# A decoder layer on one core: score fills for the maxima split between ScalarE and VectorE, the FFN's rank product in token halves

## The chip, the cores and the metric

One core of a Trainium2 chip runs the whole program. The metric is the device time of one execution in microseconds. The work is in fp32 throughout.

## The reference

Sixteen sequences of 512 tokens and 256 channels go through one decoder layer. With everything that doesn't matter here cut away, it is

```python
x = layernorm(x + attn_block(x))     # short convolution, long convolution, gate, gated MLP of 672
x = layernorm(x + xattn(x, ctx))     # 16 heads of 16: causal self-attention + attention to 64 context rows
x = layernorm(x + ffn(x))            # P = x@U1 (rank 64); H = gelu(P@V1 + b1) (1024); (H@U2)@V2 + b2

# inside xattn, per head (q and k of 16 channels, scale 1/4)
att  = where(causal, q @ k.T, -inf) * scale ;  y  = softmax(att)  @ v      # 512 x 512
attc =               qc @ kc.T      * scale ;  y += softmax(attc) @ vc     # 512 x 64
return y @ Wp + bp
```

The softmax subtracts the row's maximum, so every row of scores needs a maximum before its exponentials can be taken. The kernel makes the scores twice: once with queries in the rows, to find the maxima along the free direction (the max fills), and once with keys in the rows, with the maximum already subtracted by an extra channel of the query, to take exponentials that feed the next product (the exp fills).

## The kernel before

A front part (lines 434 to 1049, about the first 300 us) computes the projections, the short and the long convolution for all sixteen sequences. The main part then works a sequence ("batch" b) at a time: `first_block` (output projection, residual, gated MLP, layer norm), `attention`, `ffn`. No loop sets the order. Each step is an operation `plan.op(name, engines, cost, fn, prio, r=, w=, ...)` of a planner (class `Plan`, line 100). It holds a cost in microseconds for each operation, a priority (plus an offset from the table `RANKS`, line 27, by part and name), and which tiles it reads and writes. `schedule` runs a list schedule over the five engines with these costs, gives out the tiles of each pool, and `emit` issues the instructions in that order. On the chip each engine then goes through its instructions strictly in this order and waits on semaphores.

Matmuls are issued in one of four shapes of TensorE's array, written rows*columns in the profile: the whole (128*128, `FULL`), four strips of 32 columns (128*32, `STRIPS`), eight tiles of 32*64 (`ROWS`, for scores: each head has 32 rows) and eight of 64*32 (`BOTH`). Matmuls in different tiles of one shape run side by side. An operation with `flex=True` takes the whole array or strips, whichever the engine is in. `Plan.empty` (line 118) prices a change of shape; `HOLD` and `STAY` (line 1095) weigh against changing.

PSUM has eight banks of 128 x 512: one `scores` tile of four, one `av`, three `mm` (lines 1058 to 1060). All score fills of all batches use the one scores tile in turn.

`maxima(g)` (line 1472) handles a group of four heads, `g` of four groups per batch, in three fills of 512 columns for each of the four heads: query blocks 1 and 0 with their context columns, block 2 with its context and block 3's context, and block 3 alone. For batches 2 to 12 VectorE adds the causal mask in PSUM ("mask", line 1550) and reduces from PSUM ("max", line 1580). For batches 0, 1, 13, 14 and 15 (`COPIED`, line 1915) ScalarE copies all four banks into an `ex` tile ("copy", line 1525), GpSimd masks the diagonal there ("mask copy", line 1532) and VectorE reduces from the copy. In batches 0, 1 and 15 (`HALVED_MAX`) fill and copy are cut into two halves of the columns. `shifted(g)` (line 1584) turns the maxima of two groups into rows on TensorE and adds them to the queries; `sums` (line 1617) does the exp fills, the exponentials on ScalarE (line 1611), the causal triangle on GpSimd (line 1659) and the sums over keys. `divided` (line 1765) sends sums through DRAM and divides on GpSimd (lines 1804 and 1809); its numerators and inverses lie in two of three `nd` tiles.

`ffn` (line 1834): `x2T` is the transposed input; "rank" multiplies by `u1_s`, in which the 64 columns of U1 stand twice, so that `pT` (128 rows, 512 tokens) holds the ranks in both halves of its rows; "hidden" makes two blocks of 128 hidden channels at a time, one from each half of the rows; "gelu" (line 1876) takes 512 tokens of one block; "low" and "wide" are the two products back. The gelus and exponentials of the batches alternate in windows, since each needs its own table on ScalarE.

Of the kernel before, what the change touches and what calls it, by code (L numbers as in the profile page):

```python
# [8 lines left out]
F32 = mybir.dt.float32  # L9
# [18 lines left out]
    "context.sum ctx": -2000,  # L28
    "divided.num from": -400,
    "ffn.gelu": 4000,  # L30
    "ffn.hidden": -2000,
    "ffn.norm": 5000,
    "ffn.rank": -1000,
    "ffn.stats": 2000,
    "ffn.turn": -100,
    "ffn.wide": 4000,
    "first.load x": 2000,
    "first.out": -2000,
    "first.residual": -2000,
    "maxima0.max": -7000,  # L40
    "maxima1.copy": 1000,
    "maxima1.mask copy": -1000,
    "maxima1.max": -900,
    "mlp.down": 1000,
    "mlp.shift": -3000,
    "queries0.proj out": -320,
    "queries1.proj": 20,
    "queries1.proj out": -3000,
    "result.norm": 13000,
    "result.shift": 10000,  # L50
    "result.stats": 3000,
    "result.tokens": 14000,
    "shifted.max turn": 400,
    "shifted.shifted": 1000,
    "sums.exp": -1000,
    "sums.fill": -3000,
    "sums.sum": -2000,
    "sums.sum out": 2000,
    "values.ctx keys": 400,
    "values.ctx v out": 1000,  # L60
    "values.turn": -1000,
    "values.v": 100,
}
SLOT_OF = (1, 0, 2, 3)


class Buf:


    def __init__(self, cls):  # L70
        self.cls, self.seen, self.left, self.slot, self.t = cls, [], 0, None, None

# [27 lines left out]
class Plan:  # L100
# [55 lines left out]
    def matmul(self, out, weights, moving, **kw):  # L156

        rows, cols = self.now
        n = weights.shape[-1]
        for c in range(0, n, cols):  # L160
            cs = slice(c, min(c + cols, n))
            self.nc.tensor.matmul(out[cs], weights[:, cs], moving, **kw)  # L162
# [97 lines left out]
def decoder_layer(  # L260
# [60 lines left out]
    mask_qk = const.tile([P, P], F32, name="mask_qk")  # L321
    nc.gpsimd.memset(mask_qk, 0.0)
    nc.gpsimd.affine_select(
        out=mask_qk, in_=mask_qk, compare_op=ALU.is_ge, fill=NEG, base=0,
        pattern=[[-1, P]], channel_multiplier=1,
    )
# [100 lines left out]

    R8 = 8
# [5 lines left out]
    with ExitStack() as front:  # L434
# [40 lines left out]
        ramp_i = fp_.tile([P, P], I32, name="ramp_i")  # L475
        steps = fp_.tile([P, P], F32, name="steps")
        ramp = fp_.tile([P, P], F32, name="ramp")
        back = fp_.tile([P, 1], F32, name="back")
# [472 lines left out]
        u1_s = weights.tile([P, KD, 2, RANK], F32, name="u1_s")  # L951
        v1_s = weights.tile([P, NH // 2 * P], F32, name="v1_s")
        v2_s = weights.tile([P, D], F32, name="v2_s")
        v1_halves = v1.rearrange("r (p s n) -> s r p n", s=2, n=P)
        for n in range(2):
            half = bass.ts(n, RANK)
            fetch(u1_s[:, :, n, :], u1.rearrange("(k p) f -> p k f", p=P))
            fetch(v1_s[half, :].rearrange("r (p n) -> r p n", n=P), v1_halves[n])
            fetch(v2_s[half, :], v2)
        u1_s = u1_s.rearrange("p k s f -> p k (s f)")  # L960
# [110 lines left out]
        "row": tiles(kept, "row", 6, [P, T]),  # L1071
        "q": tiles(kept, "q", 11, [P, T]),
        "keys": tiles(kept, "keys", 5, [P, TC + T]),
        "kcs": tiles(kept, "kcs", 2, [P, 2, G, TC]),
        "ctx2": tiles(kept, "ctx2", 2, [CC, 2, TC]),
# [5 lines left out]
        "dk": dks,  # L1081
        "junk": tiles(kept, "junk", 1, [P, D]),
# [9 lines left out]
    for t in pool["maxes"]:  # L1092
        nc.gpsimd.memset(t, 0.0)

    plan = Plan(pool, 13890, 6870, nc, RANKS)
# [73 lines left out]
    def first_block(b, after):  # L1169
# [56 lines left out]
        if b:  # L1226
            scale_ops(y1, sq, p0, "ACT")
            zT = transposed(y1, lambda t: t, p0)
# [15 lines left out]
        for f in range(NF):  # L1244
            halves = []
            for w in (w_l1, w_l2):
                ps = Buf("mm")
                for k in range(KD):

                    def mm(e, f=f, w=w, k=k, ps=ps):  # L1250
                        plan.matmul(
                            ps.t, w[:, k, bass.ts(f, P)], zT.t[:, k, :], start=(k == 0), stop=(k == KD - 1)
# [24 lines left out]
        def mm_e(e, ps=ps):  # L1277
            for n, w in enumerate((w_l1, w_l2)):
                for k in range(KD):
                    for c in range(NT):  # L1280
                        plan.matmul(
                            ps.t[bass.ts(c, FE), bass.ts(n, P)], w[:, k, NF * P :], zT.t[:, k, bass.ts(c, P)],
# [32 lines left out]
    def attention(b, x_):  # L1315
# [3 lines left out]
        xT = transposed(x_, lambda t: t, p0)  # L1319
# [120 lines left out]
        def queries(g):  # L1440
# [29 lines left out]
            )  # L1470

        def maxima(g):

# [544 lines left out]
```

## Time and profile before

| | before |
|---|---|
| median of 3 runs | 2025.77 us (2019.52 to 2025.89) |
| profiled execution: time, span | 2020.74 us, 2018.6 us |
| mean granted TensorE clock | 0.992 |
| busy: TensorE, VectorE, ScalarE, GpSimd | 1946.6, 1320.4, 1046.4, 767.2 us |
| max reduces on VectorE, from PSUM and from copies | 311.1 us in 264, 140.6 us in 120 |
| masks on VectorE, in PSUM | 115.6 us in 132 |
| copies of scores on ScalarE | 114.3 us in 96 |
| exponentials on ScalarE | 362.7 us in 228 |

In a row of the profile, "x" is a count, "busy" the summed time of a group, "mean ns" the length of one instruction, and what follows the last bar is the idle time of the engine just before those instructions with what ended it. A line number can be that of a helper: line 162 issues most matmuls, so groups there are told apart by tiles and shapes. An fp32 matmul leaves two records.

### The profile page before, as it was taken

The numbers are of one execution on the slowest core, as the hardware profiler recorded it, in microseconds if no ns is written. First come the engines' busy times: TensorE is split into PE (matmuls) and PEld (weight loads), VectorE is DVE, ScalarE is ACT, GpSimd is POOL, SyncE is SP. The second block draws the span as 40 slices with busy tenths as digits, with TensorE's granted clock in tenths as the row PEclk, the third lists the DMA queues.
The fourth block names the chain that finished last, engine by engine and source line by source line (L and its number), as shares of the span: only waits on it lengthen the run. The fifth ranks groups of instructions, "written<-read, shape, count | busy, mean of one in ns | idle before, by whom it ended". The sixth has DMA issues, their size and how long they took to land. (4 is left out here: it accounts for less than half of the span.)

```text
span 2018.6 us, 63455 instructions
## 1 busy us (share of the span) xinstructions
PE 1946.6 (96%) x28134; PEld 864.7 (43%) x28134; DVE 1320.4 (65%) x1907; ACT 1046.4 (52%) x1478; POOL 767.2 (38%) x1036
## 2 busy tenths in 40 slices
PE   7999978999999999999999999999999999999997
PEld 4445645444444443434343434343434343434442
DVE  7987542556576757676767667676767575656564
ACT  6863521566536362636363545444444546656774
POOL 7685622243423242414242423333332324424442
PEclk9999989999999999999999999999999999999999
DMA  5375871031304131313132222222231313131200
GB/s 191 123 212 172 274 256 48 13 104 38 116 21 133 29 121 41 113 50 112 51 102 60 94 69 81 82 74 89 61 102 52 106 38 108 28 103 39 83 23 32
DMA packets 115043, 183.92 MB, mean 91 GB/s; under 512 B 13393, under 2 KB 62034, under 8 KB 114642
## 3 DMA queue, kind: packets, MB, share of 16 engines
q1 hardware_dynamic: 113234, 177.26, 27.9%
q8 instruction: 220, 3.60, 0.7%
q10 hardware_dynamic: 1536, 2.62, 0.4%
q14 instruction: 53, 0.43, 0.1%
HBM read 111.09 MB, written 68.76 MB: 89 GB/s over the span
## 5 line engine op out<-in xcount | busy, mean ns | idle before, releaser
L1611 ACT ACTIVATE ex<-scores 128x2048 f32<-128x2048 f32 (+1 forms) x228 | 362.7, 1607 | 181.3 <-PE scores L162 177.7
L1659 POOL TENSOR_SCALAR_AFFINE_SELECT ex<-ex 128x512 f32<-128x512 f32 x256 | 158.6, 634 | 498.9 <-ACT ex L1611 498.8
L162 PE MATMUL mm<-xT,w_l 128*32 128x512 f32 (+2 forms) x2940 | 316.5, 540 | 0.0
L1580 DVE TENSOR_REDUCE maxes<-scores 128x8 f32<-128x512 f32 (+4 forms) x264 | 311.1, 1220 | 4.5
L162 PE MATMUL scores<-keys,q 32*64 32x192 f32 (+5 forms) x5696 | 218.1, 407 | 9.5 <-ACT ex L1525 5.0
L162 PE MATMUL scores<-q,keys 32*64 32x256 f32 (+3 forms) x4480 | 179.9, 420 | 6.2 <-ACT ex L1611 4.8
L1548 DVE TENSOR_TENSOR scores<-scores,mask_qk 128x1024 f32<-128x1024 f32 x132 | 115.6, 875 | 106.1 <-PE scores L162 105.3
L162 PEld LDWEIGHTS scores<-keys,q 32*64 32x64 f32 x5696 | 102.9, 131 | 172.2 <-DVE maxes L1580 52.9
L162 PEld LDWEIGHTS mm<-xT,w_l 128*32 128x32 f32 (+1 forms) x2940 | 92.7, 111 | 184.6 <-issue 175.0
L162 PE MATMUL av<-ex,va 128*32 128x512 f32 (+3 forms) x2048 | 169.0, 437 | 0.1
L162 PE MATMUL mm<-w_l,gT 128*32 128x256 f32 (+1 forms) x2032 | 159.7, 381 | 0.0
L562 DVE SCALAR_TENSOR_TENSOR frow<-fmm,cw,frow 128x511 f32<-128x511 f32 x192 | 140.5, 743 | 26.0 <-ACT frow L554 21.7
L1580 DVE TENSOR_REDUCE maxes<-ex 128x4 f32<-128x512 f32 (+3 forms) x120 | 140.6, 1211 | 17.9 <-POOL ex L1532 13.7
L1804 POOL TENSOR_TENSOR nd<-nd,nd 128x1024 f32<-128x1024 f32 x30 | 71.2, 2373 | 204.5 <-DMA nd<-di 204.5
L1525 ACT COPY ex<-scores 128x1024 f32<-128x1024 f32 (+1 forms) x96 | 114.3, 1228 | 66.7 <-PE scores L162 55.9
L547 PE MATMUL fmm<-fx,inw 128*128 128x512 f32 x312 | 142.2, 598 | 0.0
L361 DVE COPY row<-av 128x512 f32<-128x512 f32 x66 | 45.6, 690 | 138.8 <-PE av L162 137.7
L1876 ACT ACTIVATE row<-mm,b_s 128x512 f32<-128x512 f32 x124 | 78.9, 685 | 102.4 <-PE mm L162 99.5
L162 PE MATMUL mm<-xT,wqc_s 128*32 128x512 f32 (+1 forms) x796 | 125.4, 595 | 0.0
L162 PEld LDWEIGHTS scores<-q,keys 32*64 32x64 f32 x4480 | 79.5, 131 | 98.6 <-ACT ex L1611 45.0
L162 PEld LDWEIGHTS mm<-w_l,gT 128*32 128x32 f32 (+1 forms) x2032 | 89.3, 117 | 68.8 <-issue 34.5
L1263 ACT ACTIVATE row<-mm 128x512 f32<-128x512 f32 x80 | 47.9, 599 | 123.7 <-PE mm L162 112.0
(201 smaller groups left out, 2954.6 us busy)
## 6 DMA issues: line engine op xcount, KB each, us to landing
dn<-row SPq DMA_DIRECT2D x120, 256.0 KB
keys<-dk SPq DMA_DIRECT2D x64, 256.0 KB
nd<-dn SPq DMA_DIRECT2D x30, 512.0 KB
nd<-di SPq DMA_DIRECT2D x30, 512.0 KB
fx<-hpad SPq DMA_DIRECT2D x28, 512.0 KB
early<-gates SPq DMA_DIRECT2D x16, 512.0 KB
early<-yconv SPq DMA_DIRECT2D x32, 256.0 KB
dk<-row SPq DMA_DIRECT2D x32, 256.0 KB
```

Source lines behind the costliest of these rows:

```text
L162: self.nc.tensor.matmul(out[cs], weights[:, cs], moving, **kw)
L361: nc.vector.tensor_copy(dst, src)
L547: nc.tensor.matmul(ps.t, inw[:, k, bass.ts(m, P)], xT.t[:, k, :], start=(k == 0), stop=(k == KD - 1))
L562: lambda e, lag=lag: nc.vector.scalar_tensor_tensor(t.t[:, lag:], ps.t[:, 0 : T - lag], cw[:, m, 2 - lag : 3 - lag], t.t[:, lag:], ALU.mul ...
L1263: lambda e, pa=pa, ge=ge: nc.scalar.activation(ge.t, pa.t, AF.Gelu_apprx_tanh),
L1525: lambda e, sc=sc, both=both, cols=cols: nc.scalar.copy(both.t[:, :, cols], sc.t[:, :, cols]),
L1548: nc.vector.tensor_tensor(diag, diag, mask, ALU.add)
L1580: nc.vector.tensor_reduce(dst, src, AX.X, ALU.max, negate=True)
L1611: lambda e: nc.scalar.activation(ex.t.rearrange("p (r n) -> p r n", r=HPG)[:, :, cols], sc.t[:, :, cols], AF.Exp, scale=scale),
L1659: lambda e, ex=ex, at=at: nc.gpsimd.affine_select(out=ex.t.rearrange("p (r n) -> p r n", r=HPG)[:, :, at : at + P], in_=ex.t.rearrange("p ...
L1804: lambda e, nums=nums, inv=inv: nc.gpsimd.tensor_tensor(nums.t, nums.t, inv.t, ALU.mult),
L1876: lambda e, f=f, s=s, bank=bank, dst=hT[s]: nc.scalar.activation(dst.t, bank(s), AF.Gelu_apprx_tanh, bias=b1_s[:, f : f + 1]),
```

## The change

In `maxima`, every batch now does the same. ScalarE copies two of the four heads (two banks) into an `nd` tile ("half"); GpSimd masks the diagonal there ("half mask"). At the same time VectorE works from the other two banks: it adds the mask to the diagonal blocks into a new small tile `part` ("mask"), reduces or folds what lies left of the diagonal into it ("off"), takes the context maxima ("max ctx"), and then, with no further use of PSUM, the own maxima from `part` ("max own") and those of the copied heads ("half ctx", "half own"). `COPIED`, `HALVED_MAX` and `SLOT_OF` go; max fills are no longer halved. `reading` tells the tile framework that the two engines read different banks, so that neither waits for the other.

In `ffn`, "rank" has U1 once and puts the first 256 tokens of a sequence into the upper half of the rows of `pT` and the last 256 into the lower half; it is always in strips. "rank out" copies 256 columns. "hidden" does a pair of channel blocks as sixteen matmuls of 256 tokens, two banks holding a token half each, and "gelu" is cut into four of 256. `v1_s` has all of V1 in both halves of its rows. The product "ctx v" of the context values makes 128 columns in strips, without the copy "twice" on GpSimd and its `ctx2` tiles. `row` tiles go from 6 to 5, `q` tiles from 11 to 10; the DMA latencies and the ranks of the planner are other numbers, and `HOLD` and `STAY` too. `turned` and the branches for `TURNED` are new code that no batch uses, since `TURNED` is empty.

```diff
-    "maxima0.max": -7000,
-    "maxima1.copy": 1000,
...
+    "maxima0.half ctx": 1000,
+    "maxima0.max own": 3000,
...
+PARTS = 1
...
-        u1_s = weights.tile([P, KD, 2, RANK], F32, name="u1_s")
-        v1_s = weights.tile([P, NH // 2 * P], F32, name="v1_s")
+        u1_s = rows(u1, "u1_s")
+        v1_s = weights.tile([P, NH * P], F32, name="v1_s")
...
-        "row": tiles(kept, "row", 6, [P, T]),
-        "q": tiles(kept, "q", 11, [P, T]),
+        "row": tiles(kept, "row", 5, [P, T]),
+        "q": tiles(kept, "q", 10, [P, T]),
...
-        "ctx2": tiles(kept, "ctx2", 2, [CC, 2, TC]),
+        "part": tiles(kept, "part", PARTS, [P, HPG // 2, 2 * P]),
...
-    plan = Plan(pool, 13890, 6870, nc, RANKS)
+    plan = Plan(pool, 13040, 5040, nc, RANKS)
...
+        def ctx_v(e, ps=ps):
+            for n in range(P // SLOT):
+                nc.tensor.matmul(
+                    ps.t[bass.ts(n, SLOT), 0:P].rearrange("p (a n) -> p a n", a=2),
+                    ctxT[:, b * TC + n % 2 * SLOT : b * TC + (n % 2 + 1) * SLOT],
+                    wcv_s.rearrange("c (a e n) -> c e a n", a=2, e=2)[:, n // 2], start=True, stop=True,
+                )
...
+            for use in (((0, TC), (1, TC)), ((2, TC), (3, None)), ((3, 0),)):
+                sc, part, half = Buf("scores"), Buf("part"), Buf("nd")
...
+                plan.op("fill", "PE", tiled(T), mm, prio, r=[q, kk], w=[(sc, 0), (sc, 1)], tiling=ROWS, urgent=True)
+                plan.op(
+                    "half", "ACT", act(two * T), lambda e, sc=sc, half=half: reading(sc, e, nc.scalar.copy(half.t, sc.t[:, two:])),
+                    prio - 6, r=[(sc, 1)], w=[half],
+                )
...
+                plan.op("half mask", "POOL", 0.4 * blocks, masked, prio - 6, w=[half])
...
+                plan.op("mask", "DVE", dve(blocks * two * P), mask, prio - 5, r=[(sc, 0)], w=[part])
+                if i0 == 0:
                     plan.op(
+                        "off", "DVE", dve(two * P),
...
+                else:
+                    reduce(
+                        "off", two * i0 * P, lambda part=part: part.t[:, :, P : P + 1],
...
+                if ctx:
+                    ctx_max("max ctx", lambda sc=sc: sc.t[:, here], here, (sc, 0), prio - 5)
...
+                        "max own", 2 * two * P, lambda: own(0, here, 2),
...
+                if ctx:
+                    ctx_max("half ctx", lambda half=half: half.t, there, half, prio - 4)
...
+                            "half own", two * n, lambda i=i: own(i, there),
...
-                plan.matmul(ps.t, u1_s[:, k, :], x2T.t[:, k, :], start=(k == 0), stop=(k == KD - 1))
-
-            plan.op("rank", "PE", pe(T), pt, p3 - k, r=[(x2T, k)], w=[ps], flex=True)
...
+                for n in range(P // SLOT):
+                    half, cols = n // 2, bass.ts(n % 2, SLOT)
...
+                        to, moving = ps.t[bass.ts(n, SLOT), 0:D], tokens(x2T, k)[:, bass.ts(half, D)]
+                    nc.tensor.matmul(to, u1_s[:, k, cols], moving, start=(k == 0), stop=(k == KD - 1))
+
+            plan.op("rank", "PE", pe(D), pt, p3 - k, r=[(x2T, k)], w=[ps], tiling=STRIPS)
...
+                for s in range(2):
+                    for c in range(0, P, SLOT):
+                        for h in range(2):
+                            half, at = bass.ts(h, RANK), (2 * fp + s) * P + c
+                            nc.tensor.matmul(
+                                bank(h)[c : c + SLOT, bass.ts(s, D)], v1_s[half, at : at + SLOT], pT.t[half, 0:D],
+                                start=True, stop=True,
+                            )
...
+                        "gelu", "ACT", act(D, True),
...
-    COPIED = (0, 1, B - 3, B - 2, B - 1)
-
-    HALVED, HALVED_MAX = (0, 1, B - 1), (0, 1, B - 1)
+    TURNED = (), (), (), ()
+
+    HALVED = (0, 1, B - 1)
```

## The prediction

> **What bounds the kernel now.** I read the page's busy table first, then the busy time by stage, then the timeline of two microseconds-long cycles in the middle, and last the groups by shape. The span of the profiled execution is 2018.6 us and its own time 2020.74 us; the median of the three timed runs is 2025.77 us. All sums below are made on 2020.74, which is 5 us under that median; about 0.3% (6 us) is what a measurement of this kernel can tell from no change.
>
> ```profile
> span 2018.6 us, 63455 instructions
> PE 1946.6 (96%) x28134; PEld 864.7 (43%) x28134; DVE 1320.4 (65%) x1907; ACT 1046.4 (52%) x1478; POOL 767.2 (38%) x1036
> ```
> ```profile
> 1000.00:1100.00 100.00, 100.00 (x1516) 41.51 (x1508) 67.73 (x97) 47.58 (x60) 33.65 (x44) 1.00 0.27 82
> 1885.00:1925.00 40.00, 36.15 (x776) 15.44 (x776) 32.98 (x37) 32.80 (x42) 17.55 (x22) 1.00 0.19 58
> ```
> In the middle (the row from 1000 us: PE, PEld, DVE, ACT, POOL, clock, DMA) TensorE is busy all 100 us at full clock, VectorE 68, ScalarE 48. Busy alone proves little, so I price its work from the timeline:
>
> ```profile
> 1001.02 1.12 PE L162 MATMUL scores<-keys,q 32*64 32x448 f32 x32
> 1002.07 0.66 PE L1591 MATMUL mm<-ident,maxes 128*128 128x128 f32 x4
> 1002.27 0.70 DVE L1548 TENSOR_TENSOR scores<-scores,mask_qk 128x512 f32<-128x512 f32 x1 [0.42 <-PE scores L162]
> 1003.00 2.36 DVE L1580 TENSOR_REDUCE maxes<-scores 128x8 f32<-128x512 f32 x2
> 1005.68 1.11 PE L162 MATMUL scores<-keys,q 32*64 32x512 f32 x16
> ...
> 1010.34 1.28 ACT L1611 ACT_TABLE_LOAD   x1 [11.40 <-DVE maxes L1580]
> ...
> 1014.09 1.12 PE L162 MATMUL scores<-q,keys 32*64 32x384 f32 x32
> ...
> 1017.43 1.12 PE L162 MATMUL scores<-q,keys 32*64 32x256 f32 x32
> ...
> 1033.00 1.04 PE L162 MATMUL mm<-xT,wk_s 128*32 128x512 f32 x8
> ...
> 1036.77 1.90 PE L162 MATMUL mm<-xT,wqc_s 128*32 128x512 f32 x16
> ```
> A matmul leaves two records, so the eight strip matmuls of a projection are x16. Sixteen records take 1.90 us, eight take 1.04: eight more cost 0.86 us, and the other 0.18 is the pipe running empty. So one k-step of 512 tokens in four strips streams 0.86 us; at 256 columns the same comparison (0.64 us for 8 records of the MLP's down product, 1.94 for 32) gives 0.43 for eight. Adding up the columns of all records at this rate gives 90 to 91 us of stream in each 100 us from 500 to 1600. The rest is the change of tile shape: the fill at 1001.02 streams 0.86 and its successor starts after 1.05 (0.19 to leave it); entering costs about 0.13. A batch lasts 104 us and has 24 fills of the scores banks, hence 24 x 0.32 = 7.7 of the 9.5 us not streamed. TensorE is really full; nothing else is close.
>
> The second resource is the one scores tile (four banks). A max fill holds it until VectorE has masked and reduced it: 1001.02 to 1005.68, 4.7 us a cycle. An exp fill cycles in 3.3 us (1014.09 to 1017.43). Twelve of each make 96 of 104 us.
>
> **The change, part by part.**
>
> *Rank product.* Before, two k-steps of 512 tokens per batch (u1 is there twice so that both halves of the rows hold the ranks); after, the same two with 256, each strip with its own tokens. 2 x (0.86 - 0.43) = 0.86 us a batch. That strips with different moving data run together is seen in the sums over keys (av from ex), which do just that at the same rate.
>
> *Context values.* One step of 256 columns becomes 128: 0.43 to 0.22, 0.21 us a batch. Together 1.08 us x 16 = **-17.3 us** of stream on the full engine. The POOL copy that it needed (16 x 0.29) goes.
>
> *Hidden and gelu.* Eight matmuls of 512 become sixteen of 256: same columns, no change. ScalarE gets 16 gelus of 256 for 8 of 512 per batch. A gelu of 512 takes 685 ns, and the slope of ScalarE is (1865 - 1015) / 1024 = 0.83 ns an element, so one of 256 is 472: +2.1 us a batch. With 48 of 100 us busy this is covered, except after the last exp, where the chain goes from hidden by gelu to the low product: two gelus 1.37, four 1.89, **+0.5**.
>
> *Maxima.* The groups:
>
> ```profile
> L1580 DVE TENSOR_REDUCE maxes<-scores 128x4 f32<-128x2048 f32 x44 | 100.9, 2293 | 1.5
> L1548 DVE TENSOR_TENSOR scores<-scores,mask_qk 128x512 f32<-128x512 f32 x88 | 61.4, 698 | 65.8 <-PE scores L162 65.8
> L1580 DVE TENSOR_REDUCE maxes<-scores 128x4 f32<-128x1024 f32 x44 | 53.5, 1215 | 0.0
> L1525 ACT COPY ex<-scores 128x1024 f32<-128x1024 f32 x72 | 69.5, 1015 | 39.0 <-PE scores L162 28.2 <-issue 10.5 <-ACT row L363 0.3
> L1532 POOL TENSOR_SCALAR_AFFINE_SELECT ex<-ex 128x512 f32<-128x512 f32 x80 | 49.7, 635 | 132.9 <-ACT ex L1525 119.6 <-PE mm L162 6.7 <-DMA nd<-di 6.5
> ```
> VectorE's fixed part is 0.15 us (681 ns for 512 elements, 1215 for 1024: 1.04 ns each). Uncopied batches (2 to 12), per head group: masks 1.23 + 2 x 0.70, reduces 7.32, sum 9.95 us in 9 instructions. After: 17 instructions, 7,172 elements, 3.74 + 3.31 + 3.01 = 10.06 us. So +0.11 a group, +0.4 a batch: nothing. In the five copied batches the masks were POOL's: 7.27 becomes 10.06, +11.2 us a batch. [...]
>
> ScalarE: 24 copies of 1.865 and 72 of 1.015 (114 us) become 192 of 1.015 (195): +5 us a batch on average, +12 in uncopied ones. POOL: 80 masks of 0.635 become 256 of about 0.41 (slope from 1024 elements at 1.09): +54 us in all. Totals: DVE 69%, ACT 57%, POOL 41%, all beside a full TensorE.
>
> The scores tile is now free after the slower of the copy (1.02) and VectorE's first half (mask 0.70, off 0.43, context 0.43: 1.56; the others 1.54 and 1.38), where it was 3.0 to 3.8. That is 12 x 1.8 = 22 us less hold a batch, and 96 becomes 74. What it gives back is only what TensorE waits for: in the middle the mean cost of a shape change lies above its median, together 0.6 us a batch. Between 0 and 0.6 x 13 = 8 us I take half, **-4**.
>
> *Where the cover is thin.* Batches 0, 1 and 15 lose their halved max fills; the halves ran back to back, so no shape change goes, and a whole fill holds the tile no longer than two copies of 1.015 did. In the last batch's maxima (row from 1885 us) VectorE is busy 33.0 of 40 us; +11.2 makes 44.2, so the stage is at least **+4.2** unless work moves out of it; ceiling 11. The first batch (maxima from 362 to 390 us, VectorE nearly full) is the same with the next batch's matmuls as filler: 0 to 9, I take **+2**.
>
> *New waits.* VectorE's half reduces stand in its queue behind POOL's mask, which stands behind POOL's 2.4 us products; behind them stand the copies that free TensorE's three mm banks. The half sits in an nd tile; a quotient trip holds two of the three. One part tile only makes VectorE wait for itself. SP's queue loses one weight load and moves nothing else. Row tiles (6 to 5) and q tiles (11 to 10) can hold back a projection; unseen in the trace, 0 to 5, I take 0. The planner's new ranks and latencies reorder all; three more or fewer shape-change pairs a batch are 16 us either way, and I take 0.
>
> Sum: -17.3 - 4 + 4.2 + 2 + 0.5 = -14.6, so 2020.7 - 14.6 = **2006 us**.
>
> **The rivals.** *A: in-order waits (slower).* POOL's long operations (two products 2.37, two sums 1.28, two biases 2.37, four others 1.28) fill about 17 of 104 us. A mask that meets one waits some 1 us: 192 x 0.17 x 1 = 33, with the nd shortage 35. If none of that is covered, TensorE's next fill waits: 2006 + 35 = 2041. It decides once over six tenths of it (21 us) reaches TensorE, 0.11 us a fill. Against: TensorE waits for scores only 0.4 us twice in two batches now, with as long an order. *B: order.* Two to three more shape changes a batch eat the stream: about 2020. For: rank is now strips only, and beside transposes that is one change more; against: 29 of its 32 k-steps were strips already (232 records of 128*32, 6 of 128*128). *C: the ends shrink too.* Between 300 and 600 us and after 1646, non-streamed time is 13 and 25 us above the middle's rate; an order that fills 15 of it gives 1991. That the split saves no stream is excluded by the av rows.
>
> **How the numbers follow.** Forecast 0.52 (2006), C 0.22 (1991), B 0.12 (2020), A 0.14 (2041). Faster by over 0.3%: 0.52 + 0.22 = 0.74; within: 0.12; slower: 0.14. C's lower end, 1985 (six more of the 38), and the forecast with +11, +9 and +5 plus no relief, 2006 + 6.8 + 7 + 5 + 4 = 2029, bound the range: 1985 to 2029 leaves out most of A and little else.
>
> **What would show it.** Right: u_s records of 256 columns at half the busy time (14 to 18 us for 31.5), stream per batch down 1 us, the batch at 103 us, fills of the max stage about 3.5 us apart, TensorE still 100% in the middle. Wrong: idle TensorE before scores fills ended by VectorE or POOL, a half mask that waits behind the products, more than 27 shape-change pairs a batch, or maxima of the last batch over 50 us.

## Result and the profile after

The changed kernel takes 2078.8 us (median; 2074.5 to 2085.1) beside 2025.8 for the kernel before on the same chip: a ratio of 1.0264, 95% interval 1.0221 to 1.0306. It is slower by about 53 us, where 2006 was forecast. The profiled execution took 2077.2 us.

The page's span and busy table, and the row of busy time from 1000 to 1100 us (PE, PEld, DVE, ACT, POOL, clock, DMA share, GB/s):

```profile
span 2075.2 us, 66287 instructions
...
PE 1951.3 (94%) x28924; PEld 866.6 (42%) x28924; DVE 1343.2 (65%) x2498; ACT 1131.6 (55%) x1683; POOL 813.4 (39%) x1196
```
```profile
1000.00:1100.00 100.00, 95.86 (x1513) 40.41 (x1514) 62.99 (x123) 57.30 (x77) 38.80 (x57) 0.98 0.25 77
```

TensorE was busy all of these 100 us before; now it idles in 4.1 of them. Its stream has shrunk as planned: the columns of all matmul records, at the 0.86 us for eight strip records of 512 that the prediction worked out (0.84 ns a column, records of tiles side by side counted once), add up to 1776.1 us before and 1758.9 after. That is -17.2 where -17.3 was forecast. What isn't streamed grew from 2018.6 - 1776.1 = 242.5 us to 2075.2 - 1758.9 = 316.3. So the loss to be explained is +73.8 us, and changes of tile shape are not it: 973 in the run before, 984 after. It is mostly waiting: TensorE is idle for 2075.2 - 1951.3 = 123.9 us where it was 2018.6 - 1946.6 = 72.0, or 51.9 more.

The timeline shows what TensorE now waits for. In a row, "[2.97 <-POOL nd L1586]" is the idle time of the engine before the instruction and what ended it. First a max fill:

```profile
1001.74 2.35 POOL L1890 TENSOR_TENSOR nd<-nd,nd 128x1024 f32<-128x1024 f32 x1 [4.96 <-DMA nd<-di]
...
1002.99 1.11 PE L164 MATMUL scores<-keys,q 32*64 32x512 f32 x16
...
1004.05 2.38 POOL L1206 TENSOR_TENSOR xt<-xt,b_s 128x1024 f32<-128x1024 f32 x1
...
1006.39 0.40 POOL L1586 TENSOR_SCALAR_AFFINE_SELECT nd<-nd 128x256 f32<-128x256 f32 x1
...
1006.83 0.95 DVE L1561 TENSOR_REDUCE maxes<-nd 128x2 f32<-128x768 f32 x1 [2.97 <-POOL nd L1586]
...
1008.03 0.95 DVE L1561 TENSOR_REDUCE part<-scores 128x2 f32<-128x768 f32 x1
...
1009.08 1.12 PE L164 MATMUL scores<-keys,q 32*64 32x192 f32 x32 [1.84 <-issue]
```

GpSimd stood 4.96 us at the quotient's product (`divide`, L1890) until the inverses landed (`nd<-di`). Behind that product came a bias add of 2.38 us, and only then the half mask. VectorE's half reduce (`maxes<-nd`, of the fill before the one at 1002.99) waited 2.97 us for that mask. What VectorE had to do for the fill at 1002.99 from its own two banks, the reduce `part<-scores` last, stood behind it in VectorE's queue; it doesn't need GpSimd at all, but it is the last reader of the scores tile. When it ended, at 1008.98, TensorE could fill again, after 1.84 us of idle. "issue" as the releaser means that the profile names nobody; the reduce's end says who it was. The second place is 70 us later. It shows the quotient's trip through DRAM, which makes GpSimd late: the denominators are loaded (`sums<-dn`, "den from" in the planner), inverted on VectorE and stored (`di<-sums`, "inverse to"); then the inverses and the numerators are loaded (`nd<-di`, "inverse from", and `nd<-dn`, "num from") for `divide`:

```profile
1062.09 0.59 SPq L1875 DMA_DIRECT2D nd<-dn  x1
...
1063.55 0.95 DVE L1865 RECIPROCAL sums<-sums 64x128 f32<-64x128 f32 x1 [2.14 <-DMA sums<-dn]
...
1064.52 0.50 SPq L1868 DMA_DIRECT2D di<-sums  x1
...
1068.53 0.59 SPq L1882 DMA_DIRECT2D nd<-di  x1
...
1075.94 2.38 POOL L1890 TENSOR_TENSOR nd<-nd,nd 128x1024 f32<-128x1024 f32 x1 [5.98 <-DMA nd<-di]
...
1079.70 2.49 POOL L1264 TENSOR_TENSOR xt<-xt,y 128x512 f32<-128x512 f32 x2
...
1082.15 1.22 POOL L1745 TENSOR_SCALAR_AFFINE_SELECT ex<-ex 128x512 f32<-128x512 f32 x2
...
1082.84 1.64 PE L164 MATMUL av<-ex,va 128*32 128x384 f32 x16 [2.30 <-POOL ex L1745]
```

The numerators' load (`nd<-dn`, 512 KB) is issued at 1062.09, the store of the inverses (`di<-sums`, 32 KB) 2.4 us behind it. The load that reads them back (`nd<-di`) goes 4.0 us after the store and lands 7.4 us later. GpSimd stands at divide for 5.98 us until then, then has the product, a sum and a residual to do, and the causal triangles that TensorE's `av` needs come last: 2.30 us of idle. Over the run TensorE's waits are:

```profile
PE av L164 <- POOL ex L1745: 19.0, 10, 3.4
PE scores L164 <- issue: 18.7, 12, 2.5
PE scores L164 <- ACT ex L1697: 12.9, 17, 1.6
```

In the same list of before the score fills' longest entries are these, and `av` never waits for the triangles:

```profile
PE scores L162 <- ACT ex L1525: 6.1, 8, 1.6
PE scores L162 <- ACT ex L1611: 5.9, 7, 1.2
```

Some short idles cost more than themselves, as the busy time around the second one shows (clock in the third column from the right):

```profile
1080.00:1083.00 3.00, 0.70 (x12) 0.16 (x8) 0.50 (x1) 1.68 (x4) 3.00 (x4) 1.00 0.76 227
1083.00:1087.00 4.00, 4.00 (x26) 2.47 (x18) 1.28 (x2) 0.72 (x2) 4.00 (x4) 0.57 0.26 89
```

After the idle of 2.30 us the granted clock is half for 3.4 of the next 4 us. The mean granted clock over the span is 0.983 where it was 0.992: (1 - 0.983) x 2075.2 = 35.3 us of clock lost against 16.1, or 19 of the 73.8. With the 51.9 us of idle that accounts for nearly all of it.

**Why the trip is late.** Part of the diff that the prediction passed over in a clause is the planner's latencies. Before, each leg of the trip was planned with 4.0 us; now sum to and den from have 1.7, inverse to 1.1, numerators and inverse from 5.7. The rank that put the numerators' load ahead of the denominators' is gone too. The new list allows 1.88 us from the store of the inverses to the load that reads them back. In the trace it is 3.3 to 4.8 us in 24 of the 30 trips (median 4.16). SyncE's queue has its waits at that load, in total, times and longest:

```profile
SPq L1882 <- DMA di<-sums: 109.1, 30, 7.4
```

The kernel's own list, with the times that the planner gave each operation, can be worked out from its code, and set beside the trace:

| | list: den from to divide, most trips | divide on the chip, mean lateness | span - 275.9 (front's list) - list's end |
|---|---|---|---|
| before | 15.7 to 16.8 us | -0.4 us | 2018.6 - 275.9 - 1743.5 = -0.8 us |
| after | 12.2 to 13.1, six of them 15.9 to 17.5 | +2.6 | 2075.2 - 275.9 - 1726.7 = 72.6 |

Lateness is the start of divide in the trace less its start in the list, both counted from ScalarE's position at that time. The chip keeps before's list to a microsecond, and falls 72.6 us behind after's.

### The profile page after: what moved, and what is told of

It is laid out like the page before. It is cut to its first block, busy times and chain, and to the rows that moved or that the text cites. A ratio compares the mean times of both kernels' runs of the same rounds, so it can differ in the third digit from the quotient of the medians.

```text
span 2075.2 us, 66287 instructions
## 1 busy us (share of the span) xinstructions
PE 1951.3 (94%) x28924; PEld 866.6 (42%) x28924; DVE 1343.2 (65%) x2498; ACT 1131.6 (55%) x1683; POOL 813.4 (39%) x1196
## 4 chain that ended last, share of the span: by engine, by line
PE 69%; DMA 13%; POOL 5%; issue 5%; DVE 4%; ACT 4%; SPq 1%; POOLq 0%; ACTq 0%; DVEq 0%
PE mm L164 32%; PE scores L164 16%; PE av L164 7%; PE fmm L582 5%; DMA nd<-di 4%; PE mm L1965 2%; DMA dn<-row 2%; ACT ex L1697 2%; PE mm L406 2%; DMA di<-sums 2%; POOL nd L1890 1%; PE fmm L842 1%; DMA sums<-dn 1%; DMA keys<-dk 1%; DMA dk<-row 1%
## 5 line engine op out<-in xcount | busy, mean ns | idle before, releaser
L1579 ACT COPY nd<-scores 128x1024 f32<-128x1024 f32 x192 | 194.6, 1014 | 304.4 <-PE scores L164 220.2
L1586 POOL TENSOR_SCALAR_AFFINE_SELECT nd<-nd 128x256 f32<-128x256 f32 x256 | 101.4, 408 | 523.8 <-ACT nd L1579 523.7
L1561 DVE TENSOR_REDUCE maxes<-nd 128x4 f32<-128x256 f32 (+4 forms) x384 | 247.0, 677 | 52.1 <-POOL nd L1586 52.1
L164 PE MATMUL scores<-keys,q 32*64 32x192 f32 (+3 forms) x5120 | 217.0, 436 | 29.5 <-issue 18.7
L164 PE MATMUL av<-ex,va 128*32 128x512 f32 (+3 forms) x2048 | 170.2, 443 | 19.2 <-POOL ex L1745 19.0
L164 PEld LDWEIGHTS scores<-keys,q 32*64 32x64 f32 x5120 | 89.4, 131 | 190.0 <-issue 111.3
L164 PE MATMUL mm<-w_l,gT 128*32 128x256 f32 (+1 forms) x2344 | 168.4, 381 | 0.0
L164 PE MATMUL mm<-xT,wqc_s 128*32 128x512 f32 (+1 forms) x874 | 123.9, 596 | 0.0
L1890 POOL TENSOR_TENSOR nd<-nd,nd 128x1024 f32<-128x1024 f32 x30 | 71.2, 2372 | 123.4 <-DMA nd<-di 123.4
L164 PEld LDWEIGHTS mm<-w_l,gT 128*32 128x32 f32 (+1 forms) x2344 | 81.1, 112 | 83.4 <-issue 43.4
L1600 DVE TENSOR_TENSOR part<-scores,mask_qk 128x256 f32<-128x256 f32 (+1 forms) x192 | 97.5, 508 | 26.9 <-PE scores L164 24.2
L1977 ACT ACTIVATE row<-mm,b_s 128x256 f32<-128x256 f32 x248 | 100.3, 476 | 26.4 <-PE mm L1965 13.3
L589 ACT ACTIVATE frow<-fmm,cb,cw 128x512 f32<-128x512 f32 x96 | 74.0, 777 | 70.3 <-PE fmm L582 52.8
```

The lines of the kernel that those rows point to most:

```text
L589: lambda e: nc.scalar.activation(t.t, ps.t, AF.Identity, bias=cb[:, m : m + 1], scale=cw[:, m, 2:3]),
L1561: inst = nc.vector.tensor_reduce(dst(), src(), AX.X, ALU.max, negate=negate)
L1579: "half", "ACT", act(two * T), lambda e, sc=sc, half=half: reading(sc, e, nc.scalar.copy(half.t, sc.t[:, two:])),
L1586: nc.gpsimd.affine_select(out=block, in_=block, compare_op=ALU.is_ge, fill=NEG, base=0, pattern=[[0, two], [-1, P]], channel_multiplier=1,)
L1600: reading(sc, e, nc.vector.tensor_tensor(to, on_diagonal(sc.t[:, here]), m, ALU.add))
L1890: lambda e, nums=nums, inv=inv: nc.gpsimd.tensor_tensor(nums.t, nums.t, inv.t, ALU.mult),
```

## The experiments

The theory: the finished order has no room for the trip, and engines that take their instructions strictly in order pay for that again and again. The first rivals: the split fills themselves cost the time, or the order does for another reason (shape changes, lack of fillers). All medians below are beside the kernel before on the same chip (2023.7 to 2025.9 us).

### Shorten or postpone the trip, keep the split

`c1_small_num` loads 32 KB of numerators instead of 512 and multiplies the inverses with themselves, so the numerators are left out of its result:

```diff
-  out=nums.t, in_=dn.t[:, 1 : 1 + HD].rearrange(...)
+  out=nums.t[:, 0, 0:64], in_=dn.t[:, 1 : 1 + HD, 0:1, 0:64].rearrange(...)
-  nc.gpsimd.tensor_tensor(nums.t, nums.t, inv.t, ALU.mult)
+  nc.gpsimd.tensor_tensor(nums.t, inv.t, inv.t, ALU.mult)
```

> The changed kernel, order of every engine untouched; the numerators' transfer back (num from, 512 KB) is cut to 32 KB and the divide multiplies the inverses with themselves, so the numerators are left out of the result. Theory (late trip): the 32 KB 'inverse to' lands some 2 us late because it goes out behind the 512 KB of 'num from'; GpSimd stands at the divide with masks and triangles queued behind it, and TensorE waits for those. Then 'inverse from' is issued about 2 us after 'inverse to' instead of 4, the divide finds its data, and the time is 2000 to 2015 us. Rival (the split itself: copy, mask and half reduces in three in-order queues): nothing of that is touched, 2065 to 2085 us.

Measured 2022.7 us, ratio 0.9987 (0.9978 to 0.9997). The store of the inverses now takes its planned time (median 1.88 us from its issue to the load behind it; SyncE's waits for it fall from 109.1 to 44.9 us). Waits of TensorE between 600 and 1646 us, first after's and then c1's (total us, times, longest):

```profile
PE scores L164 <- issue: 12.9, 9, 2.2
PE av L164 <- POOL ex L1745: 12.8, 7, 2.9
```
```profile
PE scores L164 <- issue: 2.0, 3, 0.8
PE av L164 <- POOL ex L1745: 1.7, 5, 0.4
```

`c2_no_inv` multiplies numerators by themselves, so that divide doesn't wait for the inverse (`nums.t, nums.t, nums.t`).

> The changed kernel, order of every engine and every transfer untouched; the divide multiplies the numerators with themselves, so it does not wait for 'inverse from' (the inverses are left out of the result). Late trip: GpSimd's stand at the divide is the path by which the late transfer does harm, so 2000 to 2015 us as with the small transfer. If the transfer hurt in another way (queues, SBUF), the small transfer helps and this does not: 2060 to 2085. The split itself: 2065 to 2085.

Measured 2032.6 us, 1.0037 (1.0016 to 1.0057). `c5_divide_later` computes all and moves only divide and the sum behind it back in the finished order:

```diff
+  done = self.later(done, ("divided.both", "divided.divide"), 8.0)   # up to 8 us later in the list
```

> The changed kernel with its whole result; in the finished order the two GpSimd operations 'divide' and 'both' are put behind whatever the planner starts within 8 us after them, as far as tiles and users allow; nothing else moves. Late trip: masks and triangles pass the waiting divide; most of the loss comes back, 2015 to 2040 us (projections of the result then come later). The split itself: 2065 to 2085.

Measured 2041.5 us, 1.0072 (1.0051 to 1.0094). Three ways to keep GpSimd from standing at divide end 56, 46 and 37 us below after, with the split maxima untouched in all three. So the late trip carries the loss, and the split fills don't. c1, c2 and c5 landed 8, 18 and 1.5 us above their expected bands: without the late trip the rest of the forecast isn't there yet.

`c4_ffn_alone` puts the rank product and the context values of the change into the kernel before, whose maxima, ranks and latencies stay.

```diff
-  plan.matmul(ps.t, u1_s[:, k, :], x2T.t[:, k, :], ...)
+  for n in range(4):   # strip n: its own half of the tokens, 256 columns
+      nc.tensor.matmul(ps.t[bass.ts(n, SLOT), 0:D], u1_s[:, k, cols], x2T.t[:, k, bass.ts(n // 2, D)], ...)
```

> The kernel before with the FFN's token halves (rank, hidden, gelu) and the short context values alone; its maxima, its ranks and latencies stay. The sum of the prediction, in which the stream that goes is time that goes: 17 us less, 2003 to 2013 us. Order theory: the ranks were numbers for another list of operations; the planner's own list with them ends 27 us later than that of the kernel before though TensorE streams 17 us less, so 2040 to 2056 us.

Measured 2049.9 us, 1.0127 (1.011 to 1.0143): 17 us less stream, no split, and 25 us slower. Its list ends at 1770.7 us where before's ends at 1743.5: ranks chosen for other instructions made a worse list. So this part of the change can't be read off by switching it on alone under before's ranks.

### The list's latencies

`c3_true_lat` changes four numbers in the code of after:

```diff
-  sum to lat=1.7   inverse to lat=1.1   num from lat=5.7   inverse from lat=5.7
+  sum to lat=2.2   inverse to lat=3.4   num from lat=6.2   inverse from lat=6.2
```

> Kernel after with only the assumed latencies of the quotient's trip changed to what its trace shows: sum to 2.2 us (was 1.7), inverse to 3.4 (was 1.1), numerators and inverse from 6.2 (was 5.7); den from stays 1.7, ranks, hold and stay as in after. The full result is computed. The kernel's own list then ends at 1767.1 us instead of 1726.7 (front 275.9 in both). Theory 1 (the list was laid out for a trip 3 us shorter than it is, and the engines that run it in order pay for that over and over): now list and chip agree to within 20 us, as in c1_small_num, so 2043 to 2063 us; losing 40 us in the list buys back what the chip lost, and the idle time of VectorE before the half reduces of nd and of TensorE before av behind POOL's triangles falls to less than half of after's. Rival (the split fills themselves cost the time, wherever GpSimd stands): the lag of the chip behind its list stays at 70 us, so 2110 us or more.

`c7_before_num_later` moves one step in before's order:

```diff
+  # the numerators' load goes just behind the denominators' load, in all 30 trips
```

> Kernel before with one step of its finished order moved: in each of the 30 trips the load of the numerators (512 KB) is issued just behind the load of the denominators instead of just ahead of it, as in after. Nothing else moves. Theory 1 (what counts is the room that the order leaves behind the trip, and before's order assumes 4 us for each leg): the denominators come 2 to 5 us sooner, the inverse's store takes 3.5 us or more instead of 1 to 2, divide starts within 2 us of where it did, and the time stays at 2025, within 0.5% (2015 to 2036). Rival (the 32 KB store behind the 512 KB load costs the time in any order): 2060 us or more.

`b1_ranks` is c3 with its ranks searched anew (offline, for the end of the list):

```diff
-  plan = Plan(pool, 13040, 5040, nc, RANKS)
+  plan = Plan(pool, 6962, 10412, nc, RANKS)
-  "divided.divide": 2000, "ffn.wide": -3000, "values.ctx v": -3000, ...
+  "divided.divide": 3000, "ffn.wide": 3000, "values.ctx v": -5890, "divided.num from": 3413, ...
```

> Kernel c3_true_lat (after's instructions, the measured latencies) with the ranks, hold and stay searched anew for the list's end under these latencies: the list ends at 1720.8 us, the front at 275.9. The full result is computed. Theory 1 says the chip follows a list with right latencies to within 0 to 20 us: 1997 to 2017 us, faster than before (2025) by 0.4% to 1.4%. Rival (after's instructions lose to before's in any order, through the split maxima): 2025 us or more.

| kernel | time, ratio | list: den from to divide, most trips | divide late, mean | chip behind list |
|---|---|---|---|---|
| c7 | 2025.7, 1.0004 (0.9995 to 1.0014) | 15.7 to 16.8 us | -0.4 us | 4.2 us |
| c3 | 2061.6, 1.0182 (1.0153 to 1.0211) | 15.0 to 16.3, some 19.2 | +0.8 | 16.6 |
| b1 | 2005.2, 0.9912 (0.9891 to 0.9932) | 16.8 to 18.4 | 0.0 | 8.3 |
| c1 | 2022.7 | as after | +1.3 | 18.6 |

All three times fell into their bands; two of the signs that were to come with them didn't. In c3 VectorE's waits for the half masks were to fall to less than half: they fell from 52.1 us to 38.3, while TensorE's waits for the triangles fell from 19.0 to 0.9. c3 shows that a list with the right latencies is kept to 17 us; its list ends at 1767.1 us, 40 later than after's, with ranks that were chosen under the wrong latencies. In c7 the store was to go out close behind the load and to take 3.5 us or more. It still went 5.3 to 9.3 us behind it in 29 of the 30 trips, and SyncE waited 25.0 us for it in all (24.6 in before). So c7 shows that moving the load does no harm in an order in which the store doesn't follow closely; a store close behind the load it doesn't test. b1 does: there the store goes 2.4 to 4.7 us behind the load, its way to the load behind it takes 4.4 us in the median, as long as in after, and yet TensorE hardly ever waits: the list leaves room for it, and divide isn't late. b1 computes the same, by the same operations as after, in another order, and beats both kernels. Its page, the row from 1000 us, and TensorE's waits between 600 and 1646 us, of which there is one:

```profile
span 2005.0 us, 66162 instructions
...
PE 1933.3 (96%) x28852; PEld 865.6 (43%) x28852; DVE 1336.9 (67%) x2487; ACT 1133.9 (57%) x1694; POOL 812.9 (41%) x1196
```
```profile
1000.00:1100.00 100.00, 99.14 (x1545) 41.48 (x1534) 66.16 (x129) 57.72 (x75) 38.82 (x57) 1.00 0.28 82
```
```profile
PE scores L218 <- issue: 0.8, 1, 0.8
```

### How a late quotient reaches TensorE

The two timelines name GpSimd's queue: half masks and triangles behind divide. Other routes: VectorE, which stands at the reciprocal; the three `nd` tiles, two of which a trip holds while ScalarE's half copies need one; the late rows themselves. First the two victims were moved to VectorE, at their old places in the order: `c8_masks_vector` (half masks), `c9_triangles_vector` (triangles), `c10_both_vector`.

```diff
-  nc.gpsimd.affine_select(out=block, in_=block, compare_op=ALU.is_ge, fill=NEG, ...)     # c8, c10
+  nc.vector.tensor_tensor(block, block, mask_qk.unsqueeze(1).to_broadcast([P, two, P]), ALU.add)
-  nc.gpsimd.affine_select(out=ex..., in_=ex..., compare_op=ALU.is_ge, fill=0.0, ...)     # c9, c10
+  nc.vector.tensor_tensor(ex..., ex..., tri.unsqueeze(1).to_broadcast([P, HPG, P]), ALU.mult)
```

> Kernel after, its finished order, latencies and ranks unchanged; only the half masks (256 instructions of 0.41 us on GpSimd, L1586) are computed by VectorE instead, as an add of mask_qk, at the same place of the order. The full result is computed. Queue theory (a late quotient costs time because GpSimd stands at divide while half masks and triangles stand behind it): one of the two victims is freed, TensorE's idle time before the scores fills falls, that before av behind POOL's triangles stays; 2045 to 2068 us. Rival (what costs is that the quotient itself, and the rows made from it, are late): 2072 us or more, plus what 85 us of further work on VectorE adds.

> Kernel after, its finished order, latencies and ranks unchanged; only the causal triangles of ex (256 instructions of 0.64 us on GpSimd, L1745) are computed by VectorE instead, as a product with a 0/1 triangle, at the same place of the order. The full result is computed. Queue theory: the other victim is freed, TensorE's waits for ex from POOL before av (19.0 us in 10 waits between 600 and 1646 us of after) go, the waits for the half masks stay; 2045 to 2068 us. Rival (the late quotient itself): 2072 us or more. VectorE takes some 160 us more work in both.

> Both of the above in one kernel: half masks and triangles on VectorE, so that nothing that TensorE waits for within a batch stands behind divide on GpSimd; divide still waits as late as in after for the inverse. Queue theory: most of the 55 us comes back, 2020 to 2045 us, although the quotient is as late as in after. Rival (the late quotient itself costs the time): 2070 us or more.

Measured 2069.3 (1.0227, 1.02 to 1.0254), 2092.4 (1.0344, 1.0311 to 1.0377) and 2080.6 us (1.0279, 1.0254 to 1.0303). The intervals of c8 and c10 overlap with that of after. In c8 TensorE's waits before score fills halve and those for the triangles stay, as expected, but its time lies just above its band; c9 and c10 missed the queue theory's bands and fell into their rivals'. (The 19.0 us in 10 waits that c9's expectation gives for 600 to 1646 us are those of the whole run; in that stretch they are 12.8 in 7.) TensorE between 600 and 1646 us in c8, then in c10:

```profile
PE av L164 <- POOL ex L1744: 12.4, 5, 3.1
PE scores L164 <- issue: 6.1, 8, 1.7
```
```profile
PE scores L164 <- ACT ex L1701: 11.6, 25, 0.6
PE av L164 <- DVE ex L1749: 10.3, 18, 1.1
```

In c10 TensorE waits for GpSimd nowhere in the batches any more, but the triangles now take 0.68 us each (median) in VectorE's queue, and the waits come back as many short ones. These two mixed the freed queue with a fuller VectorE and settle nothing.

`c11_nd4` gives after a fourth nd tile (and 9 q tiles for 10, to make room), `c12_nd4_masks` gives it to c8:

```diff
+  plan.more = {"nd": tiles(kept, "nd_", 1, [P, 2, T]), "q": []}   # tiles dealt again along the finished order
```

> Kernel after, its finished order unchanged, with a fourth tile in the ring nd (4 KB per partition; the ring of q shrinks from 10 tiles to 9, of which the order never holds more at a time), each tile taken by the buffer that has been free longest. The full result is computed. The trip of a quotient holds two of the three nd tiles until divide is done, and ScalarE's half copies of the scores write into the same ring: in after ScalarE waits 25.0 us in 10 waits for GpSimd's divide before such a copy. Theory of the ring (that wait is one of the routes by which the late quotient reaches TensorE): these waits fall to under 8 us and the time to 2045 to 2070 us. Rival (the tiles of nd cost nothing, the masks and triangles behind divide alone do): 2072 to 2085 us.

> c11_nd4 and c8_masks_vector in one kernel: four nd tiles, and the half masks on VectorE at the same place of the order. Theory of several routes (ring and masks both lead from the late divide to TensorE, and c8's 28.7 us of waits of ScalarE for divide were what held it): the time falls below both, 2030 to 2058 us. Rival (one route only, or the late quotient itself): no lower than the lower of c8 (2069) and c11, within 5 us.

Measured 2086.5 (1.0325, 1.0283 to 1.0367) and 2067.1 us (1.0225, 1.0205 to 1.0245), beside 1.0264 for after and 1.0227 for c8: no gain, as the rivals had it, though ScalarE's waits for divide before a half copy fell from 25.0 us to 10.0 and from 28.7 to 10.6. The ring alone is not the route. `c16_no_reciprocal` leaves the reciprocal out:

```diff
-  lambda e, sm=sm: nc.vector.reciprocal(sm.t, sm.t)
+  lambda e: None
```

> Kernel after, finished order unchanged, with the reciprocal of the denominators left out (30 instructions on VectorE of about 1 us, at which VectorE stands until the load of the denominators lands: 61.2 us in 24 waits in after), so that VectorE never waits for the trip; the store behind it waits for the load instead, and divide comes about 1 us sooner. Route by VectorE: 2030 to 2058 us. Queue theory of GpSimd (route by masks and triangles): only the 1 us by which the trip is shorter counts, 2060 to 2080 us.

Measured 2085.1 us, 1.0304 (1.028 to 1.0328). Taking away VectorE's 61 us of waiting at the reciprocal gains nothing; VectorE then waits 65.1 us for the half masks, where it was 52.1. Even the GpSimd side of the expectation (2060 to 2080) was too low. Then the victims were left out instead of moved, so that no engine gets more work: `c13_no_triangles`, `c14_queue_free` (triangles and half masks), and as control `c15_small_num_free`, which is c14 with c1's short trip.

```diff
-  "triangle": nc.gpsimd.affine_select(...)        # c13, c14, c15
+  "triangle": None
-  "half mask": nc.gpsimd.affine_select(...)       # c14, c15
+  "half mask": None
```

> Kernel after, finished order unchanged, with the causal triangles of ex left out (256 instructions on GpSimd; the later keys are then not masked in the weights). Queue theory: TensorE's waits for ex from POOL vanish and nothing takes their place, 2035 to 2062 us. Rival (the lateness reaches TensorE another way, by VectorE's queue or the late rows themselves): 2066 us or more.

> c13 with the half masks left out as well (256 more instructions on GpSimd; half of the maxima are then taken over unmasked scores). Nothing that TensorE waits for within a batch is then behind divide on GpSimd, and divide is as late as in after. Queue theory: 2005 to 2040 us, and c15_small_num_free is no more than 15 us below it. Rival (another route): 2055 us or more, and c15 lies 30 us or more below.

> The control: c1_small_num (numerators' load cut to 32 KB, divide from the inverse alone, so a short trip) with the same triangles and half masks left out as in c14. c1 took 2022.7 us. Leaving out two short instructions in the chains shortens them, so 2005 to 2022 us. If c1 to c15 is as much as after to c14, what c14 gains is not the standing behind divide but the missing instructions; the queue theory expects after to c14 to be larger by 30 us or more.

Measured 2082.9 (1.0287, 1.0255 to 1.032), 2039.6 (1.0069, 1.0046 to 1.0092) and 2012.9 us (0.9945, 0.9928 to 0.9962). Leaving out the triangles alone gives nothing, and c13 fell into its rival's band: between 600 and 1646 us TensorE's waits for them (12.8 us) are gone, but those before score fills rise from 12.9 us to 18.6, and 5.6 us of waits for the rows made after the quotient (`y`) are new. The half masks alone were only moved (c8, some 10 us), not left out. Both together give 39 us. The control gives 2022.7 - 2012.9 = 10 for the shorter chains alone, so about 30 us belong to standing behind divide in GpSimd's queue, if the shorter chains are worth as much in c14 as in the control. c14 still lies 27 us above its control, between the two theories' bounds. ScalarE's waits for divide before a half copy are its most visible difference from the control, where they are 6.2 us in 3. `c17_queue_free_nd4` gives c14 the fourth tile. These waits in c14, then in c17:

```profile
ACT nd L1579 <- POOL nd L1881: 44.9, 15, 6.0
```
```profile
ACT nd L1595 <- POOL nd L1897: 9.9, 4, 3.3
```

> c14_queue_free (triangles and half masks left out, trip as late as in after, 2039.6 us) with the fourth nd tile of c11_nd4 (the ring of q 9 tiles instead of 10), order unchanged. Theory of two routes in parallel (GpSimd's queue and the nd ring, either of which alone hides what taking the other away would give): ScalarE's waits for divide before a half copy fall from 44.9 us to under 15, and the time to 2012 to 2028 us, near the control with a short trip (2012.9). Rival (the rest is the late rows of the quotient themselves): 2033 to 2046 us.

Measured 2034.9 us, 1.0039 (1.0024 to 1.0054). The waits for the ring go, the time falls by 5 us at most (the intervals touch). About 20 us stay above the control, and the time lies in the rival's band. In c17, and in c14 too (8.3 us in 11), TensorE waits for the rows made after the quotient before it transposes them (`y`), which c15's list doesn't have at all:

```profile
PE mm L421 <- ACT y L408: 6.8, 10, 1.8
```

That points at the late rows themselves, but 7 or 8 us are less than 20, and no experiment took this wait away; this part stays open.

## Why the prediction was wrong

**The stream** (-17.3): right, -17.2. The records of the rank product:

```profile
L1943 PE MATMUL mm<-xT,u_s 128*32 128x256 f32 x256 | 20.5, 401 | 0.0
```

28.3 + 3.2 us became 20.5 and not the 14 to 18 that the prediction gave as a sign. 20.5 us are 0.64 for each of the 32 k-steps, which is what the prediction itself read for 8 records of 256 columns standing alone; 0.43 of it is stream, and the busy time counts the end as well.

**Copies, masks, gelus, maxima on VectorE**: right in size.

```profile
L1579 ACT COPY nd<-scores 128x1024 f32<-128x1024 f32 x192 | 194.6, 1014 | 304.4 <-PE scores L164 220.2
...
L1586 POOL TENSOR_SCALAR_AFFINE_SELECT nd<-nd 128x256 f32<-128x256 f32 x256 | 101.4, 408 | 523.8 <-ACT nd L1579 523.7
```

Copies 1014 ns (1015 foreseen), half masks 408 (0.41 us), and gelus of 256 tokens 476 (472). The 17 VectorE instructions of a head group (the reduces of L1561, 515.1 us in all forms, L1600's 97.5 and L1606's 27.1, over 64 groups) take 10.0 us, where 10.06 was worked out.

**Relief of the scores tile** (-4) and **the last batch** (+4.2, at most 11): the relief can't be seen beside the new waits. From its first to its last max fill the last batch took 35.3 us before (1885.1 to 1920.4), 48.6 after and 43.6 in b1. So +13 and +8: twice the term in b1, within its ceiling, and above the ceiling in after, where the waits are in it. **The first batch** (+2, 0 to 9): from 300 to 600 us, 41.1 us were not streamed before, 44.2 in b1 and 52.3 in after, again with the waits.

**New waits, taken as 0: the step that failed.** The measured time lies 2078.8 - 2006 = 72.8 us above the forecast, and c1, which changes the trip alone, takes back 56 of them. The paragraph named the right places: half reduces behind GpSimd's mask, masks behind the 2.4 us products, two of three nd tiles held by a trip. It took GpSimd's queue as late by the length of its own products and didn't ask when divide's input lands. And it took "new ranks and latencies" as able to change the number of shape changes only. A latency in a list is a promise about the trace, and before's trace could have been held against it: there the store takes 1.81 to 1.89 us to the load behind it in 13 of 30 trips, with the numerators' load issued over 7 us ahead. In those 13 trips that load's semaphore is complete 5.8 to 6.8 us after its issue, so it had landed. In after it is issued 2.4 us ahead of the store, and the list still allows 1.88.

**Rival A** (0.14, 2041 us) had the place, and two of the listed signs came: idle TensorE before score fills, and half masks behind the products; the last batch's maxima, at 48.6 us, stayed just under the 50 named. Its cause was the length of the products, at 35 us uncovered. In c1 the same products stand in the same order and TensorE's waits for the triangles between 600 and 1646 us are 1.7 us: the length alone is nearly harmless. Its price left out the triangles (19.0 us of waits) and the clock (19 us). **Rival B**, more shape changes, is out: 984 for 973. **Rival C**, shorter ends, didn't come in after; after 1646 us the time not streamed is 90.9 us where it was 66.5.

**The gain itself was real.** In an order that leaves the trip its time (b1), the same operations take 2005.2 us, about what was forecast for after. Its profiled execution streams 1758.9 us of 2005.0, so 246.0 are not streamed where before had 242.5: the gain is the 17.2 us of shorter stream less 3.5 us of the rest, where the prediction's other terms add up to +2.7. That is a fit of the size, not a proof of each term: b1's order is another one, and no run gives the kernel before ranks searched anew, so how far a new search alone would carry it isn't known. Of the 17 us by which c1 stays above the forecast only part is traced, to a divide that is still 1.3 us late.

## What to carry to other kernels

Where a static list orders in-order engines, check every latency that a change puts into it against the trace of before, transfer by transfer and with what is queued ahead: 3 us too little on one trip cost more than the 17 us that the change saved. A wait matters by what stands behind it on its engine, and where two victims stand behind one wait, freeing one of them may show nothing (c13) and both much (c14). And compare a change only with ranks found anew for it: c4 and c3 lost 25 and 37 us to before although they stream 17 us less.

## What the runs showed of the hardware that was not expected

A 32 KB store issued mostly 2 to 3 us behind a 512 KB load held up the load that waits for it to 4.16 us after the store's issue (median of after), where it is 1.88 us with a 32 KB load in the large one's place (c1). The two have the same order; only the size of the load and the operands of divide differ. In b1, whose list has room for it, it is 4.4 us.

TensorE's granted clock fell to half for 3.4 or 6.8 us after idles of 1.9 to 5.2 us (from 1.5 us before their end to 1.3 us behind it), nine times between 400 us and the last matmul of after (some 41 us at half clock; once, 3.4 us, in before, behind an idle of 1.60 us), and not after others of 1.8 to 2.5 us. In after an idle of 1.86 us was followed by a drop of 3.4 us and one of 2.52 us by none, so the length of the idle alone doesn't tell which brings one; no run here shows what else decides it.
